# Layer 0's attention over all four quarters as one chain, the following layers behind it by quarters, and layer 2's attention on rows gathered one by one

## The chip, the core and the metric

The kernel runs on one core of one Trainium2 chip. The metric is the device time of one execution in microseconds (us). The kernel before has a median of 2545.66 us over 11 runs (2534.57 to 2553.08).

## The reference

Four layers, each an attention and a feed-forward part, over x of 4 batch rows, 1024 time steps, 128 channels, fp32. Every part is followed by the residual and a layer norm: x = layernorm(x + f(x)). Cut to what the change touches:

```python
def L0_attn(x):                       # a linear attention by cumulative sums over time
    z = causal_conv(x @ in_proj_w) + conv_b              # values, scores, gate
    p_w = exp(clip(score)) * time_weight
    poly = w[0] + w[1]*xv - w[2]*xv**2
    re, im, den = cumsum([p_w*poly*cos(xv*theta), p_w*poly*sin(xv*theta), p_w], axis=time)
    ...                               # / den, rms norm over 2*H*M, W_re, W_im
    return (y * gate) @ out_proj_w
def L0_ffn(x):  return dequant(fp6_blocks32(x)) @ dequant(fp6_blocks32(weight)).T + bias
def L1_attn(x): h[t] = a_disc*h[t-1] + B_disc @ x[t]; return Re(C @ h)      # complex state
def L1_ffn(x):  # 16 experts, 4 per token chosen by groups, beside a shared expert
    return sum_k(tw[k] * expert[idx[k]](x)) + shared(x)
def L2_attn(x): # 16 heads of 8, rotary, softmax over the earlier steps of the same row
    return softmax(mask(q @ k.T)) @ v @ Wo
def L2_ffn(x):  # 8 experts with low-rank additions to common weights, 2 per token
...
```

All that carries over time (the sums of L0_attn, the state of L1_attn, the causal mask of L2_attn) needs earlier steps of the same row first. Routing of a token needs only the token.

## The kernel before

x stays in SBUF as 32 tiles of 128 tokens by 128 channels, ordered by quarter: a quarter is 256 time steps of all four batch rows, 8 tiles. Two quarters are a half.

The program is written as Python generators that issue instructions and yield a nominal duration. `mix(main, side, pace, drain)` (L233) runs two of them against each other: after each step of main it advances side until the nominal times match, and ties each side instruction behind main's latest one on its engine. `press` (L1796) runs a side until something is ready; `chain` and `abreast` put generators one behind the other or next to each other; `all` (L1809) is the order of stages. A scheduler in the framework then fixes the order within each engine. Every engine works through its own list in order and waits at the first instruction that isn't ready. SP issues the plain DMAs in order, POOL the indirect DMAs, in one list with its tensor work.

Stages up to the part that the change leaves alone, in order:

- `l0_attn((0, 1))` (L362): per quarter a projection and convolution on PE, polynomial and phases on DVE and ACT, 9 cumulative scans per quarter on DVE (`l0_scan`, L352), output projection, `norm` (L185). The products with the polynomial run on POOL here (L442), on DVE in quarters 2 and 3 (`no_pool`).
- `l1_setup` (L545), which depends on weights alone, `l2_setup`, `zero_lists` (zero rows to DRAM), and `l0_ffn((0, 1))` (L501) with `quantize` (L473), whose steps alternate DVE and POOL.
- `l1_attn((0, 1))` (L620: projections, two scans, output projection, norm, transposes) beside `l2_weights` (L1385), which builds the 24 weight blocks of the layer-2 experts on PE and stores them to DRAM (`wall2`).
- `l1_route(a)` (L744): scores, top 4, and the position of every token in the lists of its experts (`posl1a`, L1270).
- `l0_attn((2, 3))` beside `spread("l1", a)` (L1305). `spread` is a scatter: for each of 16 tiles and each of its 4 choices one indirect DMA on POOL writes 128 rows of x into the list `l1ra` in DRAM, 64 in all.
- `l1_experts(a)`: 20 groups of 512 list rows are loaded by SP (`xg`), transposed, multiplied by the weights of their expert (`gu`, then `yp`), and stored. `l0_ffn((2, 3))` and `l1_attn((2, 3))` lie beside.
- `l1_shared(a)` and the rest of that side, beside `l1_close(a)` (L825): `collect` (L1348) gathers each token's 4 results (`yt`, indirect DMAs on POOL), adds them, then norm, a store to `xsave`, transposes.
- `l2_attn(0)` (L880), the first half of layer 2's attention by batch rows (`prepare(b)`, scores `sc`, exponentials `pr`, products `s`), beside `l1_route(r)` and `spread("l1", r)` for the second half (list `l1rr`).
- `l1_experts(r)` and `l1_shared(r)` beside `routed(a2)`, layer 2's own routing and scatter (list `l2ra`, 32 scatters); then `l2_experts(a2)` beside `l1_close(r)`; then `l2_attn(1)` and the rest of layers 2 and 3.

The weights of the layer-1 experts, 3 MB (`l1_wall`, L1655), are loaded twice, ahead of `l1_experts(a)` and ahead of `l2_attn(0)`; the second copy stays until `l1_experts(r)` is done.

The core of `spread`, for each tile `t`:

```python
for i in range(k):
    ins = self.indirect(apart=done,
        out=rows, out_offset=bass.IndirectOffsetOnAxis(ap=pos[:, t, i : i + 1], axis=0),
        in_=self.x[:, part.order[t], :], in_offset=None)
```

## Time and profile before

| | |
|---|---|
| median of 11 runs | 2545.66 us (2534.57 to 2553.08) |
| the profiled execution | 2544.01 us |
| its span on the core | 2542.1 us |
| busy: PE, weight loads, DVE, ACT, POOL | 1696.9, 1031.4, 1348.7, 810.7, 779.4 us |
| mean granted TensorE clock | 0.822 |
| HBM read and written | 93.47 and 96.60 MB, 75 GB/s over the span |

Where the stages lie in the trace, by their first and last instructions:

| stage | us from the start |
|---|---|
| `l0_attn` of quarters 0 and 1 | 24 to 154 |
| `l0_ffn` of 0 and 1 | 154 to 207 |
| `l1_attn` of 0 and 1, `l2_weights` | 207 to 285 |
| `l1_route(a)` | 285 to 313 |
| `l0_attn` of 2 and 3, `spread` of `l1ra` | 313 to 428 |
| `l1_experts(a)` | 428 to 541 |
| shared, `l1_attn` of 2 and 3, `l1_close(a)` | 541 to 657 |
| `l2_attn(0)`, `l1_route(r)`, `spread` of `l1rr` | 657 to 921 |
| `l1_experts(r)`, `spread` of `l2ra` | 936 to 1047 |
| `l1_shared(r)` | 1047 to 1089 |
| `l2_experts(a2)`, `l1_close(r)` | 1089 to 1247 |
| `l2_attn(1)` | 1247 to 1660 |
| the rest | 1660 to 2542 |

Busy time is time in which an engine executes something; PE is the matrix engine and PEld its weight loads, DVE the vector, ACT the scalar and POOL the general engine. L12 is line 12 of the kernel before. A name like `gu<-ld,xgT` is what an instruction writes and reads. A wait on "remote" or "another core or an unknown queue" is one whose releaser the profile can't name; there is only one core here.

### The profile page before, as it was taken

The page shows a single profiled execution, that of the slowest core. Times are in us where ns is not written, and L with a number is a line of the kernel's source. Part 1 is how long each engine was busy: PE and PEld are TensorE (multiplying, and loading weights), DVE is VectorE, ACT ScalarE, POOL GpSimd, SP SyncE. Part 2 cuts the span into 40 slices and gives each one's busy share as a digit, 9 for nine tenths or more (in the row PEclk, how much of TensorE's full clock was granted, in tenths as well). Part 3 has the DMA queues.
Part 4 walks back from the last instruction along what each step waited for, and adds up shares of the span by engine and source line. Part 5 has one row for each costly group of instructions (what it writes and reads, how often), then busy time and mean ns, then how long its engine had stood idle before and what let it go on. Part 6 is the DMA issues. An engine that isn't in the chain of part 4 may idle for free.

```text
span 2542.1 us, 28615 instructions
## 1 busy us (share of the span) xinstructions
PE 1696.9 (67%) x9605; PEld 1031.4 (41%) x9605; DVE 1348.7 (53%) x3797; ACT 810.7 (32%) x1158; POOL 779.4 (31%) x725
## 2 busy tenths in 40 slices
PE   7538676873551884797797878768619896754820
PEld 3225333752320353655432332335416684542710
DVE  8864795856460662344546673735403576641453
ACT  5512362311230441222365545512102352310310
POOL 5432185225135004223220001020560203154364
PEclk9768787986785997898898989978859997886965
DMA  9902002341001133322300000030410331221422
GB/s 318 289 14 86 17 35 100 104 133 41 22 25 42 52 120 115 92 60 58 112 24 1 1 3 15 14 126 24 174 58 17 102 108 43 89 87 53 116 79 53
DMA packets 224008, 192.05 MB, mean 76 GB/s; under 512 B 16817, under 2 KB 204081, under 8 KB 222833
## 3 DMA queue, kind: packets, MB, share of 16 engines
q1 hardware_dynamic: 203152, 147.28, 18.4%
q0 software_dynamic: 20704, 42.86, 5.5%
q8 instruction: 83, 1.36, 0.2%
q14 instruction: 69, 0.56, 0.1%
HBM read 93.47 MB, written 96.60 MB: 75 GB/s over the span
## 4 chain that ended last, share of the span: by engine, by line
PE 38%; DVE 15%; another core or an unknown queue 11%; issue 7%; ACT 3%; DMA 2%; POOL 2%; SPq 0%; POOLq 0%; DVEq 0%; ACTq 0%
PE gu L157 10%; PE s L157 8%; PE sc L157 5%; PE yp L157 5%; PE tp L165 4%; PE pu L157 2%; PE pg L157 2%; PE py L157 2%; DVE x L1359 1%; DVE pr L1055 1%; POOL yt L1293 1%; ACT pr L1049 1%; POOL l3rb L1293 1%; DVE x L205 1%
## 5 line engine op out<-in xcount | busy, mean ns | idle before, releaser
L1049 ACT ACTIVATE pr<-sc 128x1024 f32<-128x1024 f32 x288 | 279.5, 1021 | 318.3 <-PE sc L157 200.5
L157 PE MATMUL gu<-ld,xgT 128*128 x768 | 206.6, 412 | 51.7 <-ACT xgT L167 16.9
L157 PE MATMUL s<-pr,va 128*32 128x512 f32 (+3 forms) x1536 | 179.0, 531 | 45.9 <-issue 27.7
L157 PE MATMUL sc<-qm,kT 32*128 32x512 f32 (+3 forms) x1536 | 197.1, 557 | 10.8 <-ACT pr L1049 6.3
L157 PE MATMUL gu<-wall,xgT 128*128 x352 | 181.0, 641 | 20.2 <-DMA wall<-wall 18.2
L157 PEld LDWEIGHTS gu<-ld,xgT 128*128 128x128 f32 x768 | 148.1, 204 | 84.6 <-ACT xgT L167 29.1
L165 PE MATMUL tp<-ld,hg 128*128 128x128 f32 x736 | 117.6, 281 | 90.9 <-DVE hT L169 50.9
L169 DVE COPY hT<-tp 128x512 f32<-128x512 f32 x140 | 96.0, 686 | 139.2 <-remote 68.4
L165 PEld LDWEIGHTS tp<-ld,hg 128*128 128x128 f32 x736 | 93.9, 146 | 149.0 <-issue 62.5
L1689 DVE TENSOR_TENSOR hg<-sg,gu 128x256 f32<-128x256 f32 x192 | 78.5, 417 | 126.2 <-ACT sg L1688 108.5
L1462 ACT ACTIVATE sg<-gu 128x512 f32<-128x512 f32 x88 | 52.5, 597 | 284.4 <-PE gu L157 161.5
L1055 DVE TENSOR_TENSOR pr<-pr,ld 128x512 f32<-128x512 f32 (+1 forms) x160 | 92.4, 580 | 93.1 <-ACT pr L1049 90.5
L157 PEld LDWEIGHTS sc<-qm,kT 32*128 32x128 f32 x1536 | 84.4, 198 | 113.5 <-issue 70.0
L167 ACT COPY xgT<-tp 128x512 f32<-128x512 f32 x118 | 69.1, 586 | 178.0 <-PE tp L165 127.0
L165 PE MATMUL tp<-ld,xg 128*128 128x128 f32 x472 | 77.8, 290 | 69.8 <-ACT hT L167 24.3
L1688 ACT ACTIVATE sg<-gu 128x256 f32<-128x256 f32 x192 | 72.8, 384 | 161.9 <-PE gu L157 111.3
L1464 DVE TENSOR_TENSOR hg<-sg,gu 128x512 f32<-128x512 f32 x88 | 60.1, 682 | 107.6 <-ACT sg L1462 93.1
L1293 POOL DMA_INDIRECT l1ra<-x,posl1a x64 | 93.9, 1468 | 61.0 <-DVE posl1a L1270 41.8
L1293 POOL DMA_INDIRECT yt<-l1yr,posl1r x64 | 60.5, 945 | 152.7 <-DVE x L1359 79.5
L157 PE MATMUL yp<-ld,hT 128*128 x768 | 103.1, 276 | 3.6 <-DVE hT L169 3.3
L157 PEld LDWEIGHTS s<-pr,va 128*32 128x32 f32 x1536 | 38.8, 113 | 157.1 <-issue 111.2
L157 PE MATMUL yp<-wall,hT 128*128 x704 | 98.2, 285 | 1.5 <-DVE hT L169 1.5
(433 smaller groups left out, 3531.9 us busy)
## 6 DMA issues: line engine op xcount, KB each, us to landing
wall<-wall SPq DMA_DIRECT2D x16, 768.0 KB
l3ra<-zero SPq DMA_DIRECT2D x1, 6144.0 KB
wall<-we SPq DMA_DIRECT2D x24, 256.0 KB
ld<-in_l_w SPq DMA_DIRECT2D x2, 3072.0 KB
ld<-in_l_w SPq DMA_DIRECT2D x1, 6144.0 KB
xg<-l3ra SPq DMA_DIRECT2D x24, 256.0 KB
l3ya<-yg SPq DMA_DIRECT2D x24, 256.0 KB
l1ra<-zero SPq DMA_DIRECT2D x1, 5120.0 KB
```

Source lines behind the costliest of these rows:

```text
L157: return self.nc.tensor.matmul(out, lhsT, rhs, start=start, stop=stop)
L165: nc.tensor.transpose(pt[:, k * P : (k + 1) * P], s, self.ident)
L167: nc.scalar.copy(dst, pt[:, : n * P])
L169: nc.vector.tensor_copy(dst, pt[:, : n * P])
L205: nc.vector.tensor_scalar(x, x, mv[:, t, 0:1], rstd[:, t : t + 1], ALU.subtract, ALU.mult)
L1049: nc.scalar.activation(pr, sc[h], AF.Exp)
L1055: nc.vector.tensor_tensor(d, d, cst["tril"].unsqueeze(1).unsqueeze(1).to_broadcast([P, 2, n, P]), ALU.mult)
L1293: ins = self.nc.gpsimd.indirect_dma_start(**kw)
L1462: nc.scalar.activation(sg, gu[:, 0, :], AF.Silu)
L1464: nc.vector.tensor_tensor(h, sg, gu[:, 1, :], ALU.mult)
L1688: nc.scalar.activation(sg, pg[:, :, 0, :], AF.Silu)
L1689: nc.vector.tensor_tensor(h[:, 2 * c : 2 * c + 2, :], sg, pg[:, :, 1, :], ALU.mult)
```

## The change

- `l0_attn` runs once, over all four quarters. Its products run on POOL in quarters 0 to 2 and on DVE in quarter 3. Behind each quarter of it, and beside the next, come `l0_ffn` and `l1_attn` of the same quarter (`after`, `then`); `l1_setup`, `l2_setup` and `zero_lists` come behind quarter 0.
- After `l1_attn` of quarter 1 comes `l1_route(a1)`, then `spread` of it abreast with `l0_ffn` and `l1_attn` of quarters 2 and 3 and `l1_route(r)`.
- What of that is left over runs beside `l2_weights`, which has its scaled copy `am` made by ACT in place of POOL. Then `l1_shared(a1)` and `l1_experts(a1)` run beside `spread` of `r`.
- `l2_attn(0)` runs beside `l1_close(a1)`, which now goes by batch rows: four tiles are gathered, added, normed, stored and transposed, and the row is listed. `prepare(b)` presses the side until its row is listed. `l1_close(r)` goes by rows too, beside `l2_experts(a2)` as before.
- The second load of the layer-1 weights comes after `l2_attn(0)`.
- The scaling of the norms of layer 0 and of `l1_attn` is on ACT (`on_act`); the reciprocal root of the `l0_ffn` and `l1_attn` norms is always on DVE. `im` and `re` take the place of `t` and `k`, three buffers each. Some pools have fewer buffers or lie on another side of SBUF.

```diff
@@ -122,7 +122,7 @@
         self.lists, self.route = {}, {}
-        self.both = (self.first, Part("r", 2, 2))
+        self.both = (Part("a", 0, 2, range(B)), Part("r", 2, 2, range(B)))
         for lay, ne, k in (("l1", E1, K1), ("l2", E2, K2), ("l3", E3, K3)):
...
@@ -201,8 +202,14 @@
                 self.rsqrt(rstd, ve)
+        if on_act:
+            off = self.tile(self.small, [P, n], f"off{n}")
+            nc.vector.scalar_tensor_tensor(off, mv[:, :, 0], -1.0, rstd, ALU.mult, ALU.mult)
         for t, x in enumerate(tiles):
-            nc.vector.tensor_scalar(x, x, mv[:, t, 0:1], rstd[:, t : t + 1], ALU.subtract, ALU.mult)
+            if on_act:
+                nc.scalar.activation(x, x, AF.Identity, bias=off[:, t : t + 1], scale=rstd[:, t : t + 1])
+            else:
+                nc.vector.tensor_scalar(x, x, mv[:, t, 0:1], rstd[:, t : t + 1], ALU.subtract, ALU.mult)
...
@@ -411,9 +418,9 @@
                 ts(pq, xv, self.nw2, self.dw[:, 1:2], ALU.mult, ALU.add)
-                times(pq, pq, xv, ALU.mult)
+                times(q)(pq, pq, xv, ALU.mult)
                 nc.vector.scalar_tensor_tensor(pq, pq, self.dw[:, 0:1], pwx, ALU.add, ALU.mult)
-                den = self.tile(bp, [P, QC], "den")
+                den = self.tile(bp, [P, QC], "den", bufs=1)
                 self.l0_scan(den, pwx, 2 * MF, q)
...
@@ -428,18 +435,18 @@
-                    t = self.tile(tp, [P, QC], "t")
-                    nc.scalar.activation(t, xv, AF.Copy, scale=self.turn[:, m : m + 1])
-                    k = self.tile(tp, [P, QC], "k")
+                    turn = self.turn[:, m : m + 1]
+                    t = self.tile(tp, [P, QC], "t", bufs=3)
+                    nc.scalar.activation(t, xv, AF.Copy, scale=turn)
+                    k = self.tile(tp, [P, QC], "k", bufs=3)
                     ts(k, t, RND, None, ALU.add)
                     nc.vector.scalar_tensor_tensor(k, k, RND, t, ALU.subtract, ALU.subtract)
-                    im = self.tile(tp, [P, QC], "im")
+                    im, re = t, k
                     nc.scalar.activation(im, k, AF.Sin, scale=-2.0 * PI_IN)
                     nc.scalar.activation(k, k, AF.Abs)
-                    re = self.tile(tp, [P, QC], "re")
                     nc.scalar.activation(re, k, AF.Sin, scale=-2.0 * PI_IN, bias=self.halfpi)
                     for part, v in ((1, im), (0, re)):
-                        times(v, v, pq, ALU.mult)
+                        times(q)(v, v, pq, ALU.mult)
                         s = self.tile(tp, [P, QC], "s", bufs=3)
...
@@ -466,7 +473,8 @@
                     tt(x[:, t0 : t0 + 4, :], po, x[:, t0 : t0 + 4, :], ALU.add)
-                self.norm(self.quarter(q), by="act" if no_pool else "pool")
+                self.norm(self.quarter(q), by="act" if q in no_pool else "pool", on_act=True)
+                self.listed.add(f"l0 {q}")
                 yield (10.0,)
...
@@ -520,7 +527,7 @@
                 )
-                yield (10.0,)
+                yield (13.0,)
...
@@ -660,7 +667,7 @@
-                (tt if beside else nc.gpsimd.tensor_tensor)(rows(g[0]), rows(g[0]), steps(pw[:, 0, :]), ALU.mult)
+                tt(rows(g[0]), rows(g[0]), steps(pw[:, 0, :]), ALU.mult)
                 tt(rows(g[1]), rows(g[1]), steps(pw[:, 1, :]), ALU.mult)
...
@@ -671,17 +678,17 @@
                     yield (3.0,)
-                self.norm(self.quarter(q), by="dve" if beside else "act")
+                self.norm(self.quarter(q), by="dve", on_act=True)
                 yield (6.0,)
-    def logits(self, pl, wr, t0, nt):
-        for t in range(nt):
-            self.mm(pl[:, t, :], self.xT[:, (t0 + t) * P : (t0 + t + 1) * P], wr)
+    def logits(self, pl, wr, tiles):
+        for i, t in enumerate(tiles):
+            self.mm(pl[:, i, :], self.xT[:, t * P : (t + 1) * P], wr)
...
@@ -824,16 +831,21 @@
-        nc, x = self.nc, self.x
-        for q in range(part.q0, part.q0 + part.nq):
-            yield from self.collect("l1", part, K1, yp, (q - part.q0) * QT, QT)
-            self.norm(self.quarter(q))
-            tl = slice(q * QT, (q + 1) * QT)
-            nc.sync.dma_start(out=self.xsave[:, tl, :], in_=x[:, tl, :])
-            yield (6.0,)
-            for g in range(2):
-                self.turned(self.side, q * QT + g * 4, tag="s")
-                yield (1.5,)
+        nc, x, hf = self.nc, self.x, part.q0 // 2
+        xTv = self.xT.rearrange("p (q b t) -> p b q t", q=NQT, b=B)
+        for b in range(B):
+            yield from self.collect("l1", part, K1, yp, b * 4, 4)
+            tiles = part.order[b * 4 : b * 4 + 4]
+            self.norm([x[:, t, :] for t in tiles], by="dve")
+            for t in tiles[::2]:
+                nc.sync.dma_start(out=self.xsave[:, t : t + 2, :], in_=x[:, t : t + 2, :])
+            yield (5.0,)
+            pt = self.tile(self.side, [P, BLK], "s")
+            for k, t in enumerate(tiles):
+                nc.tensor.transpose(pt[:, k * P : (k + 1) * P], x[:, t, :], self.ident)
+            nc.vector.tensor_copy(xTv[:, b, 2 * hf : 2 * hf + 2, :], pt.rearrange("p (q t) -> p q t", q=2))
+            self.listed.add(f"row {hf}{b}")
+            yield (2.0,)
...
@@ -909,6 +921,7 @@
+                self.press(side, lambda: f"row {hf}{b}" in self.listed)
                 qT = self.tile(bp, [P, BLK], "qT")
...
@@ -1387,16 +1400,18 @@
         with ExitStack() as ctx:
-            cp = self.pool(ctx, "l2wc", right=True)
-            wp = self.pool(ctx, "l2ww", 3, right=True)
+            cp = self.pool(ctx, "l2wc")
+            wp = self.pool(ctx, "l2ww", 3)
             big = self.load(cp, self.ins["l2_big"])
             ab = self.load(cp, self.ins["l2_ab"])
+            em = self.tile(cp, [P, E2], "em2")
+            nc.vector.tensor_scalar(em, self.cst["em"], 2.0, None, ALU.mult)
             yield (0.0,)
                     am = self.tile(wp, [P, P], "am")
-                    nc.gpsimd.tensor_scalar(am, ab[:, i, :], self.cst["em"][:, e : e + 1], 2.0, ALU.mult, ALU.mult)
+                    nc.scalar.activation(am, ab[:, i, :], AF.Copy, scale=em[:, e : e + 1])
                     pw = self.tile(self.side, [P, F2], "s")
...
@@ -1409,7 +1424,7 @@
                     nc.sync.dma_start(out=self.wall2[:, c0 : c0 + F2], in_=we)
-                    yield (1.0,)
+                    yield (2.5,)
...
@@ -1754,6 +1769,16 @@
+    def after(self, q):
+        yield from self.when(lambda: f"l0 {q}" in self.listed)
+        if q == 0:
+            self.l1_setup()
+            yield (20.0,)
+            self.l2_setup()
+            self.zero_lists("l1")
+            yield (4.0,)
...
@@ -1818,38 +1843,37 @@
                 self.l2_wr = self.load(lgp, self.ins["l2_wr"])
-                self.run(self.l0_attn((0, 1)))
-                self.l1_setup()
-                self.l2_setup()
-                weights = self.l2_weights()
-                next(weights)
-                self.zero_lists("l1")
-                self.run(self.l0_ffn((0, 1)))
-                self.run(self.mix(self.l1_attn((0, 1)), weights))
-                self.run(self.l1_route(a))
-                self.run(self.mix(self.l0_attn((2, 3), True), self.spread("l1", a, K1)))
+                main = self.l0_attn(range(NQT), (NQT - 1,))
+                then = lambda q: self.chain(self.after(q), self.l0_ffn((q,)), self.l1_attn((q,)))
+                side = self.chain(
+                    then(0), then(1), self.l1_route(a1),
+                    self.abreast(self.spread("l1", a1, K1), self.chain(then(2), then(3), self.l1_route(r))),
+                )
+                self.run(self.mix(main, side, pace=0.8, drain=False))
                 self.zero_lists("l2", "l3")
+                self.run(self.mix(self.l2_weights(), side))
                 with ExitStack() as c2:
                     wall = self.l1_wall(c2)
-                    yp = self.pool(c2, "l1ya", 5, right=True)
-                    side = self.chain(self.l0_ffn((2, 3), True), self.l1_attn((2, 3), True))
-                    self.run(self.mix(self.l1_experts(a, wall), side, drain=False))
-                    self.run(self.mix(self.chain(self.l1_shared(a), side), self.l1_close(a, yp)))
+                    side = self.spread("l1", r, K1)
+                    self.run(self.mix(self.chain(self.l1_shared(a1), self.l1_experts(a1, wall)), side))
+            with ExitStack() as c2:
+                yp = self.pool(c2, "l1ya", 5, right=True)
+                side = self.l1_close(a1, yp)
+                self.run(self.mix(self.l2_attn(0, side), side))
             with ExitStack() as c2:
                 wall = self.l1_wall(c2)
-                self.run(self.mix(self.l2_attn(0), self.chain(self.l1_route(r), self.spread("l1", r, K1))))
                 wall2 = self.l2_wall(c2)
                 self.run(self.mix(self.chain(self.l1_experts(r, wall), self.l1_shared(r)), self.routed(a2)))
-                self.run(self.mix(self.l2_experts(a2, wall2), self.l1_close(r, yp)))
+                side = self.l1_close(r, yp)
+                self.run(self.mix(self.l2_experts(a2, wall2), side))
             listed = lambda name: lambda: name in self.listed
             )
-            self.run(self.mix(self.l2_attn(1), on, drain=False))
+            self.run(self.mix(self.l2_attn(1, on), on, drain=False))
             with ExitStack() as c3:
```

The lines left out pass these things through: pool sides and names, `side` PSUM in place of own pools in `l0_ffn` and `l1_attn`, the logits by the part's tile order.

## The prediction

> **What bounds the kernel now.** I read the page's slices and chain first, then windows by stage, then the groups of the three scatter tiles, then the waits of the one stretch where all engines stand still.
>
> ```profile
> PE   7538676873551884797797878768619896754820
> DVE  8864795856460662344546673735403576641453
> POOL 5432185225135004223220001020560203154364
> PE 38%; DVE 15%; another core or an unknown queue 11%; issue 7%; ACT 3%; DMA 2%; POOL 2%; SPq 0%; POOLq 0%; DVEq 0%; ACTq 0%
> ```
>
> A slice is 63.6 us. No engine is full for long: stages with different limits follow each other. The thirteenth slice (763 to 826) has PE 1, DVE 0. "Unknown queue" holds 11% of the chain. The windows are columns of time, length, then busy us and count for PE, weight loads, DVE, ACT, POOL, then granted clock, DMA share, GB/s:
>
> ```profile
> 24.00:154.00 130.00, 85.14 (x347) 37.85 (x345) 104.07 (x118) 66.60 (x81) 57.26 (x24) 0.80 0.85 241
> 154.00:207.00 53.00, 16.12 (x69) 12.46 (x69) 34.52 (x93) 5.20 (x11) 20.21 (x11) 0.60 0.00 0
> 313.00:428.00 115.00, 78.25 (x340) 36.56 (x336) 100.55 (x146) 59.23 (x68) 93.51 (x64) 0.81 0.14 52
> 541.00:657.00 116.00, 42.92 (x161) 27.15 (x161) 60.26 (x220) 10.08 (x17) 65.98 (x64) 0.63 0.26 82
> 745.00:822.00 77.00, 9.73 (x36) 3.07 (x28) 1.93 (x7) 2.22 (x3) 51.31 (x54) 0.52 0.12 46
> 921.00:1047.00 126.00, 85.47 (x533) 74.33 (x525) 56.68 (x213) 36.62 (x74) 30.65 (x32) 0.86 0.45 147
> ```
>
> Rows 1 and 3 are l0_attn, bound by DVE. Rows 2 and 4 (l0_ffn; l1_shared, l1_attn(2,3), l1_close) are chains that fill no engine; the change wants to put these under other work. Row 5 is l2_attn(0) while spread(r) scatters: the core stands still. The groups of the scatters, l1ra (beside l0_attn(2,3)), l1rr (beside l2_attn(0)), l2ra (beside l1_experts(r)):
>
> ```profile
> L1293 POOL DMA_INDIRECT l1ra<-x,posl1a x64: 954/1043/3016, 312.6 to 424.8; - x64
> L1293 POOL DMA_INDIRECT l1rr<-x,posl1r x64: 954/958/1113, 731.7 to 811.5; - x64
> L1293 POOL DMA_INDIRECT l2ra<-x,posl2a x32: 954/958/982, 956.3 to 995.5; - x32
> ```
>
> Min/median/max ns, then first and last start. l1ra is stretched to (424.8-312.6)/63 = 1.78 us apart and costs its neighbour nothing; l1rr goes at (811.5-731.7)/63 = 1.27 us and stops everything from 745 to 822. The chain and the waits of 740 to 830 name it:
>
> ```profile
> 761.94 59.93 another core or an unknown queue
> ACT pr L1049 <- remote: 73.7, 2, 71.9
> DVE t L169 <- remote: 60.0, 1, 60.0
> ```
>
> l2ra does the same to the experts: 20 groups of l1_experts(r) take 936.2 to 1046.8 = 110.6 us, at 3.54 us a group in the undisturbed part plus 5 us run-in (76), so 32 scatters lose 34 us, about 1.1 each. l3ra (64, some 70 us lost) agrees. Two things set l1ra apart, and the trace can't part them: DVE is 99% busy from 330 to 400, and few instructions run (340 matmuls in 115 us against 533 in 126).
>
> **The change part by part.** I carry all to one mark: the first gu matmul of l1_experts(r), at 936.2 before. What comes after holds the same work (row-wise l1_close(r) and pressed waits in l2_attn(1) I put at 0, from -10 to +10: l1_close(r) lay beside l2_experts, PE 137.04 of 158 us, and still does).
>
> 1. *To posl1a.* The first quarter of l0_attn is alone as before and ends near 117. From there to posl1a (L1270), the list positions that the scatters need, the built order has 232 us of DVE work by median row durations, row by row. In parts, which come to 237: three quarters of l0_attn (45 each: scans L358 2.3, L435 1.6), l0_ffn and l1_attn of quarters 0 and 1, route(a1) (windows: 34.5+35.2+23.2 = 93), l1_setup, which lay in DVE's idle prologue (+15), g[0] on DVE (L663; 1.2 each), rsqrt on DVE (+9), less the norm scalings that go to ACT (L205, 2.14 per quarter, 8 quarters = 17). POOL's multiplies stretch DVE: in 24 to 154 the DVE rows sum to 111.6 us where their medians give 90.8. q1 and q2 keep them: +20. At 97% busy: 117 + 252/0.97 = 377; I take 375 (355 if inflation is nil and packing full, 397 if DVE is busy only 90%). Before: 312.3. The routing comes 63 us later because l0_attn(2,3) now lies ahead of it.
>
> The Trainium skill, "SBUF — State Buffer", section "Who interferes with whom", speaks against POOL multiplies beside a full DVE: the pair of ports that the two share is an exclusive lock, and the loser waits for the whole instruction. Were POOL's 57.26 us in the first window all lost to DVE, the +20 would be some +57; the measured inflation, 20.8 us, decides here. The same section says TensorE and ScalarE never wait for that lock, which taken alone would price the scatters at nothing for PE and give the fast rival below; the fifth window has PE at 9.73 of 77 us, so the measurement differs and decides.
>
> 2. *spread(a1).* POOL is in order. Its queue holds 21 scatters mixed with quantize(2) of l0_ffn, then 43 in a row, and only then quantize(3). 64 x 1.26 = 81 us, +10 for quantize(2)'s POOL rows (L485 2.2, L495 2.4, L497 2.4, L525 2.6), up to +10 for the rest of l0_attn on DVE: it ends at 466 to 476. Before, it lay wholly under l0_attn(2,3).
>
> 3. *What waits behind it.* quantize(3), stuck behind the 43, 16 to 21 us; l0_ffn(3)'s matmuls 14; norm and transposes 16; l1_attn(3) 30 (before, L641 to L672 per quarter). On PE the gu of l1_experts(a1) stand behind l1_attn(3) and route(r)'s logits. So the first gu is some 78 after 468 = 546 if nothing freezes. If the 43 freeze the tail (norms, l1_attn(2), l2_weights, whose 65 us of PE were to be filler here), 574: 28 of the 47 us they can take are on that chain. I take 562, the middle and 2 for the landing of the last scatter; before, 438.1.
>
> 4. *l1_experts(a1) beside spread(r).* 76 as above, + 64 scatters at 2 x 34 = 68, + 5 for posl1r at its head: 149. Without a freeze 85. On SP its first xg load, which waits for all of l1ra, stands ahead of six of the 24 stores of wall2 (L1411), and the 3 MB wall load behind the second group's; wall2 is read only at the mark, so the stores cost 0, and a late wall 0 to +10, in the range.
>
> 5. *Row 0 of l1_close(a1)* is pressed before l2_attn(0)'s first prepare, so nothing covers it: landing 2.3 + 16 gathers at 1.25 = 20, + adds, norm, transposes 3 to 12, + 11 to the first sc: 36. The other rows lie beside attention.
>
> 6. *l2_attn(0).* Before 668.8 to 921 = 252; less the 77 us stall that leaves it = 175; +10 for row closes on DVE (L1359, L205) = 185.
>
> 7. *To the mark.* 15 us tail as before (921 to 936.2), plus the wall: its SBUF is free only when l2_attn(0) ends, while before it was loaded ahead; 3 MB at the 14.20 us the later wall load shows: +15. In all 30. The 6 MB of wall2 follow behind it on SP; xg loads queue with it: 0 to +10.
>
> Sum: 562 + 149 + 36 + 185 + 30 = 962 against 936: **+26**. Said as a ledger: the experts start 124 us later (562 against 438), and from there to the mark takes 400 instead of 498. The profiled execution took 2544.0 (span 2542.1), 1.7 below the median of the runs; 2545.7 + 26 gives 2571 or 2572; I write 2571.
>
> The rest at 0: norm scalings and am on ACT (L1688's 128x256 takes 0.384 us, so eight 128x128 take at most 3.1 against DVE's 2.14; ACT is busy 59 of 115 us in l0_attn, 10 of 116 in the chains); sin and cos in place with three buffers, same instructions; tiles in another order in logits, lists and closes; xsave in 16 stores of 2 tiles, SP being idle; l2_attn's transposed rows copied by DVE (L169, 0.7 us each, inside term 6). If ACT were the bound the norms would cost 1 us a quarter.
>
> **The rivals.**
>
> A, *no freeze: faster.* The freeze is tied to what l2_attn and the experts happened to do; scatters run stretched beside the tail and beside the experts as l1ra did. Then 546 + 85 + 36 + 185 + 30 = 882, -54: 2491. For: l1ra's 64 without loss; l2_weights fills PE. Against: l2ra froze this very expert loop. Half of it (only spread(r) freezes, 546 + 149) is +10: 2556. It turns to a gain when the first gu comes before 536 with spread(r) frozen, or 600 without.
>
> B, *both freeze whole, POOL's queue decides: slower still.* 574 + 149 + 36 + 185 + 30 = 974, +38: 2584; with DVE only 80% busy as in the first window (104.07 of 130), posl1a comes at 117 + 252/0.8 = 432, all of 57 later: up to 2640. For: that window is the only stretch with POOL multiplies. Against: it waited for loads (DMA share 0.85), and side work fills later gaps.
>
> C, *the wall load is not exposed and rows close under cover:* SP prefetches, pressing finds row 0 ready: -30, 2541, no change within the noise.
>
> **How the numbers follow.** Forecast (partly frozen, 2550 to 2600): 0.42. B beyond 2600: 0.14. A (2470 to 2530): 0.28. C and mixtures (2530 to 2550): 0.16, of which 0.06 lies within 0.2% (5 us, about what a measurement here can tell), 0.06 below, 0.04 above. So faster 0.34, same 0.06, slower 0.60. The range leaves out the faster end of A (0.10) and the slower end of B (0.09): 2485 to 2620; the forecast's own is 2550 to 2600.
>
> **What would show it.** posl1a between 355 and 397; the last l1ra scatter near 470 with qt of quarter 3 right behind it on POOL; first gu of gu<-ld,xgT near 562; a window over l1rr with PE under 2 tenths beside the experts; l2_attn(0) without a still stretch, some 185 long; a wait on the wall near 15 us ahead of l1_experts(r). Wrong, if scatters in the tail or in the experts stand 1.7 us or more apart with PE busy, or if DVE has gaps of 20% in l0_attn. Stages behind the mark that differ by over 10 us would be a cause I haven't priced.

## The result and the profile after

The changed kernel takes 2696.8 us (median of 8 runs, 2689.3 to 2700.6) against 2544.6: a ratio of 1.0591, interval 1.0574 to 1.0609. The forecast was slower by 26 us, with a range up to 2620; it is slower by 152. The profiled execution took 2699.1, its span is 2697.3.

The slices of the page after (67.4 us each; the rows are PE, DVE, POOL):

```profile
PE   7666542683535677478779788867836898564720
DVE  6998762553244666234453666453711377550453
POOL 4533028205342100422331001002162201335264
PE 40%; DVE 21%; another core or an unknown queue 17%; issue 10%; POOL 5%; ACT 3%; DMA 3%; SPq 0%; DVEq 0%; POOLq 0%; ACTq 0%
```

The hole that lay in slice 13 of the kernel before is now spread over slices 7 (404 to 472), 10 and 12. In the chain the unknown queue rose from 11% to 17%. By windows (columns as before: us, then busy and count of PE, weight loads, DVE, ACT, POOL, clock, DMA share, GB/s), cut at the terms of the sum:

```profile
117.00:391.00 274.00, 167.48 (x699) 87.37 (x698) 220.65 (x530) 111.70 (x163) 60.66 (x24) 0.79 0.06 18
390.00:483.00 93.00, 14.99 (x50) 10.46 (x50) 23.31 (x58) 5.41 (x12) 73.69 (x68) 0.52 0.11 45
483.00:597.00 114.00, 94.84 (x399) 58.70 (x400) 61.54 (x172) 45.23 (x101) 9.12 (x5) 0.89 0.28 99
597.00:768.00 171.00, 82.76 (x477) 73.08 (x477) 58.58 (x210) 35.51 (x72) 61.91 (x64) 0.73 0.26 81
768.00:845.00 77.00, 11.52 (x20) 4.59 (x20) 25.50 (x87) 0.00 (x0) 49.47 (x52) 0.52 0.19 50
845.00:1033.00 188.00, 139.06 (x1164) 66.04 (x1165) 121.47 (x349) 75.70 (x78) 13.42 (x12) 0.85 0.08 27
```

In order: l0_attn behind its first quarter, with the layers beside it, up to the first scatter; spread(a1), with PE 15 of 93; the tail to the experts' first gu; l1_experts(a1) with spread(r) in it, PE 83 of 171; the exposed close of row 0, PE 12 of 77; l2_attn(0), no longer with a still stretch. The scatters' groups (min/median/max ns, first and last start):

```profile
L1306 POOL DMA_INDIRECT l1ra<-x,posl1a x64: 954/958/1973, 390.6 to 482.2; - x64
L1306 POOL DMA_INDIRECT l1rr<-x,posl1r x64: 954/958/1199, 621.5 to 701.7; - x64
```

l1ra's median is down from 1043 ns to 958: beside l0_attn they were held apart, here they go back to back. The waits from 620 to 715, beside spread(r), look like those of the still stretch before, at a new place:

```profile
DVE hg L1704 <- ACT sg L1703: 55.3, 3, 43.8
PEld gu L157 <- issue: 42.7, 2, 37.8
ACT sg L1703 <- remote: 34.7, 4, 12.9
```

PE's longest wait is for nothing that the profile can name ("issue"), ACT waits for an unnamed releaser, and DVE for ACT. The scatters themselves are not late: the first packet of most of l1rr's comes 1.54 us after the issue, in the middle of the stop as at its ends, and 2.6 us at most.

### The profile page after: what moved, and what is told of

Its sections match the earlier page's. It is cut to its first block, busy times and chain, and to the rows that moved or that the text cites. A ratio compares the mean times of both kernels' runs of the same rounds, so it can differ in the third digit from the quotient of the medians.

```text
span 2697.3 us, 28800 instructions
## 1 busy us (share of the span) xinstructions
PE 1725.5 (64%) x9605; PEld 1046.9 (39%) x9605; DVE 1378.1 (51%) x3887; ACT 839.9 (31%) x1254; POOL 762.4 (28%) x709
## 4 chain that ended last, share of the span: by engine, by line
PE 40%; DVE 21%; another core or an unknown queue 17%; issue 10%; POOL 5%; ACT 3%; DMA 3%; SPq 0%; DVEq 0%; POOLq 0%; ACTq 0%
PE gu L157 11%; PE s L157 10%; PE sc L157 5%; PE yp L157 5%; PE tp L165 4%; POOL yt L1306 2%; DVE s L365 2%; PE pu L157 1%; DVE x L1372 1%; PE pg L157 1%; DVE bn L192 1%; POOL l3rb L1306 1%; ACT pr L1062 1%; DVE pr L1068 1%
## 5 line engine op out<-in xcount | busy, mean ns | idle before, releaser
L157 PE MATMUL sc<-qm,kT 32*128 32x512 f32 (+3 forms) x1536 | 203.1, 574 | 12.8 <-issue 8.0
L157 PE MATMUL s<-pr,va 128*32 128x512 f32 (+3 forms) x1536 | 170.8, 526 | 14.1 <-DVE x L1000 5.3
L1479 DVE TENSOR_TENSOR hg<-sg,gu 128x512 f32<-128x512 f32 x88 | 59.9, 682 | 102.6 <-ACT sg L1477 89.7
L1306 POOL DMA_INDIRECT yt<-l1ya,posl1a x64 | 62.9, 983 | 138.9 <-issue 83.4
L157 PE MATMUL yv<-s,wbd 128*128 128x512 f32 x128 | 73.5, 701 | 40.6 <-DVE s L365 23.3
```

The source lines that it names most:

```text
L157: return self.nc.tensor.matmul(out, lhsT, rhs, start=start, stop=stop)
L1306: ins = self.nc.gpsimd.indirect_dma_start(**kw)
L1479: nc.vector.tensor_tensor(h, sg, gu[:, 1, :], ALU.mult)
```

## The experiments

### The same scatters left out of both kernels

In `spread`, the inner loop runs over nothing for the named lists; all else stays. First group of runs:

```diff
-            for i in range(k):
+            for i in range(0 if lay + part.name in ('l1a', 'l1r',) else k):    # a_no_both, b_no_both
+            for i in range(0 if lay + part.name in ('l1r',) else k):           # a_no_r
```

> The changed kernel with the 64 scatters of spread(r) left out (its list stays zero; every other instruction stays). Theory 1, scatters issued back to back stop the other engines: l1_experts(a1) took 171 us from its first gu matmul (596.8) to the first gather (768.0) where 20 groups at 3.54 us and 5 us of run-in are 76; with 5 us for the routing at its head, 90 us go: 2697 - 90 = 2607 us (2595 to 2620), and the window of the experts has PE at 8 tenths or more throughout. Theory 2, the loss lies in the new order (POOL's queue, row 0 of the close, the late wall), and the scatters fill time in which the experts wait for something else: less than 20 us go, 2680 to 2697.

> The changed kernel with the 128 scatters of spread(a1) and spread(r) left out. Theory 1: the 90 us of spread(r), and with spread(a1) gone quantize of quarter 3 no longer stands behind 64 scatters on POOL and nothing stops: the first gu matmul comes some 100 us after posl1a at 390 (end of l0_attn, quantize 19, matmuls 14, norm and transposes 16, l1_attn 30, logits and load 15), near 495 in place of 597; 2697 - 90 - 100 = 2507 us (2490 to 2530). Theory 2: l2_weights and the chain of quarter 3 fill that time anyway, and the first gu comes no earlier than 560; 2640 to 2660.

> The kernel before with the same 128 scatters left out, so that the two orders can be compared without them. Theory 1: l1ra's 64 cost nothing beside l0_attn(2,3) and l1rr's 64 cost the still stretch in l2_attn(0): 2544 - 75 = 2469 us (2458 to 2482). Theory 2, the still stretch is a wait for something that the scatters only accompany: 2535 to 2545. The difference to the changed kernel without them is what the order costs by itself: 38 us by theory 1, 100 or more by theory 2.

Measured, one run each: 2261.4, 2223.9 and 2157.4, where the kernel before took 2165.7 on that chip, some 380 below its executions on every other. Nothing stops there. l2ra's 32 scatters beside l1_experts(r), in b_no_both on that chip and then in the kernel before (b_same) on the next one:

```profile
851.00:892.00 41.00, 38.14 (x242) 34.51 (x243) 19.95 (x46) 17.52 (x37) 31.12 (x32) 0.96 0.66 199
```
```profile
954.00:995.00 41.00, 15.06 (x69) 11.98 (x69) 5.11 (x15) 4.47 (x9) 30.74 (x32) 0.74 0.35 113
```

POOL does the same (32 in 41 us, 31 busy); PE is busy 38 us on one chip and 15 on the other, and 15.8 in b_no_both2 further down, the program of the first row on a chip with the stop. So the program alone does not make the stop. Whether it is the chip or the moment these runs can't tell: all that lack it are of one group on one chip. My numbers had supposed a stop that is absent there, so the expectations of these three failed. What they do give is that the order has a price without any stop, 2223.9 - 2157.4 = 66 us, and that spread(a1) has one too: 2261.4 - 2223.9 = 37.5 us. Its scatters, and the first POOL step of quantize for the four quarters, with them (a_no_r) and without (a_no_both):

```profile
L1306 POOL DMA_INDIRECT l1ra<-x,posl1a x64: 955/962/2412, 388.8 to 483.3; - x64
L493 POOL TENSOR_TENSOR qt<-x,qri x4: 1912/1920/1926, 133.3 to 484.3; 128x1024 f32<-128x1024 f32 x4
```
```profile
L493 POOL TENSOR_TENSOR qt<-x,qri x4: 1909/1911/1912, 132.5 to 447.3; 128x1024 f32<-128x1024 f32 x4
```

quantize(3) starts right behind the last scatter, 37 us later than without, and the first gu comes 35 us later (577.4 against 541.9). That is POOL's queue, as step 3 of the prediction had it, with no engine stopped. All later groups fell on chips with the stop (before: 2544.2 to 2547.1), where I repeated the pair:

> The changed kernel without its 128 scatters of layer 1, on this chip. With the freeze: 2690 less the 95 us that l1_experts(a1) lost and less 35 to 100 us from spread(a1) to the first gu: 2495 to 2560. Its distance to the kernel before without the same scatters is the price of the order: 66 on the chip without a freeze (2223.9 against 2157.4), so 50 to 90 here. Without the freeze: 2220 to 2228 again.

> The kernel before without the same 128 scatters, on this chip. With the freeze: 2544 - 75 - 9 = 2460 (2450 to 2475), the 9 being what they cost where nothing stops (2165.7 against 2157.4). Without: 2155 to 2160.

2549.6 and 2462.2: **the order costs 87 us, with no layer-1 scatter in either.** The scatters cost 2547.1 - 2462.2 = 85 in the kernel before. In the changed one they cost 138: it stands 140.6 above the kernel before with them (a_same, below) and 2.6 without. 87 + 53 = 140. These are single runs, and the kernel before alone spreads from 2534.6 to 2553.5 over 31, so each of these differences is known to some 10 us.

Where the two kernels without scatters part (from their traces, changed against before): first gu 539.4 against 434.9; first sc of l2_attn(0) 707.5 against 663.9, +44; its last sc +64; last store of l1_experts(r) +71; first sc of l2_attn(1) 1265.7 against 1178.9, +87; after that nothing.

### The changed kernel on a chip with the stop, and two single edits

> The kernel before itself, to have its trace on this chip. If there is no freeze: 2160 to 2170, with l1rr's 64 scatters dense (1.26 us apart) and PE over 7 tenths busy beside them. If there is: 2535 to 2555 and the still stretch of 75 us.

> The changed kernel itself, beside the kernel before on the same chip. The first group of runs showed the kernel before at 2165.7 us with no still stretch around its scatters, 379 us below the recorded executions. If this chip is like that one: theory 1 (the freeze is the chip's or the moment's, the order has a price of its own) says the changed kernel is near a_no_r's 2261, since spread(r) then lies under the experts: 2255 to 2285, ratio 1.04 to 1.055. Theory 2 (the loss is the freeze) says a ratio of 0.98 to 1.02. If this chip is like the recorded one: 2690 to 2700, ratio 1.059.

2546.8 for the kernel before, and 2685.1 for the changed one (ratio 1.0554, 1.052 to 1.0589), close to the recorded result. Which scatters cost what: with and without them, the first gu comes at 593.1 and 539.4 (+54; in the kernel before 440.8 and 434.9, +6), and from there to the last store of l1_experts(a1) it takes 166.7 and 87.3 (+79; in the kernel before l2_attn(0) carried +78). So spread(r) costs the same at either place, and 48 of the extra 53 are spread(a1), which lost its cover.

```diff
 a_qdve:  -  nc.gpsimd.tensor_tensor(...)    # L493, L503, L505, L532
          +  (nc.gpsimd if q < 2 else nc.vector).tensor_tensor(...)
 a_muls:  -  main = self.l0_attn(range(NQT), (NQT - 1,))
          +  main = self.l0_attn(range(NQT), (1, 2, 3))
```

> The changed kernel with the POOL steps of l0_ffn (three in quantize, one bias add) on DVE for quarters 2 and 3, so that POOL has nothing behind or between the 64 scatters of spread(a1). Theory 1 (the chain of quarter 3 waits in POOL's queue): the scatters end 64 x 1.27 = 81 us after posl1a in place of 92 to 95, quantize(3) runs during them, and the first gu comes 40 to 75 us earlier without a freeze; with the freeze 10 to 30 us earlier, since the chain stands still anyway. Theory 2 (the tail is bound by DVE and by the 65 us of PE work of l2_weights): within 10 us of the changed kernel.

2692.3 in a single run: no gain. The scatters end 7 us sooner (474.4 against 481.6), but the first gu is at 596.9 against 593.1. With the stop POOL's queue does not decide: in the changed kernel POOL stands idle for 18.5 us behind the last scatter, until DVE has done its part of quantize(3) ("POOL qt L493 <- DVE qri L490: 18.5"). Queue and stop overlap: where nothing stops, the queue alone makes 35 of the 54 us.

> The changed kernel with the 18 products of quarters 1 and 2 of l0_attn on DVE in place of POOL (9 per quarter, 1.21 us each on DVE by the row of L442 = 22 us more DVE work, less the 20 us of inflation that I put on DVE for them). Theory 1 (POOL's products stretch DVE as much as they save): posl1a within 10 us of the changed kernel's and the time within 10 us. Theory 2 (POOL's products are nearly free): 15 to 25 us slower.

2680.1 in a single run, within what a_same's runs spread over (2677.0 to 2693.9), but the first scatter comes at 372.4 in place of 388.9. The windows up to the experts' first gu, by which both have done the same work, a_same and a_muls:

```profile
0.00:593.00 593.00, 352.86 (x1426) 187.81 (x1426) 396.53 (x853) 226.73 (x351) 202.42 (x133) 0.77 0.30 93
```
```profile
0.00:579.00 579.00, 347.13 (x1427) 188.22 (x1428) 386.53 (x871) 229.81 (x355) 142.36 (x113) 0.78 0.31 96
```

DVE does 18 products more, 22 us by their rows, and is busy 10 us less. So the 18 products on POOL, 52 us by their rows there, stretched DVE by about 32. Theory 1, and beyond it: for DVE they cost more than they saved. The rule of the Trainium skill, "SBUF — State Buffer", section "Who interferes with whom", on the exclusive lock between the two engines would, taken as a loss of all their time, give 52; the measured 32 lies between that and my +20.

### Scatters held apart

A power of a tiny tile after each scatter keeps POOL from issuing the next one; it is tied behind the scatter, and the next scatter behind it (cut to the loop; `slow` says whether the list is one of those held apart, `nap` is the last power):

```diff
                 done.append(ins)
+                if slow:
+                    if nap is not None:
+                        self.tc.add_manual_dep(ins.ins, nap.ins.name, behind, reason="paced")
+                    nap = self.nc.gpsimd.tensor_tensor(self.idle, self.idle, self.mhalf[:, :4], ALU.pow)
+                    self.tc.add_manual_dep(nap.ins, ins.ins.name, behind, reason="paced")
-            yield (1.26 * k,)
+            yield ((2.4 if slow else 1.26) * k,)
```

> The kernel before with all 64 scatters of spread(r), each followed on POOL by a tiny power of 4 elements per partition, so that they go some 2.2 to 2.6 us apart (the nominal step of spread is raised to 2.4 to match). Theory 1a, only scatters issued back to back stop the engines: 64 x 2.4 = 154 us lie beside the 175 us of l2_attn(0), no still stretch, 2544 - 70 = 2474 us (2462 to 2490). Theory 1b, each scatter costs the others about 1.1 us whatever the distance: 2540 to 2555.

2205.3, on the chip without the stop, which both theories miss; it decides nothing, as told in the next one:

> The kernel before with l1rr's 64 scatters held 2.4 us apart by a tiny POOL power after each, again, since the first such run fell on a chip where back-to-back scatters stop nothing (2205.3 against 2165.7 for the kernel before: there the longer spread only ended 41 us after the attention). On a chip with the freeze (before near 2545): theory 1a, only back-to-back scatters stop the engines: l2_attn(0) has no still stretch and the spread ends some 40 us after it: 2544 - 75 + 41 = 2510 (2495 to 2525). Theory 1b, each scatter costs some 1.1 us at any distance: 2560 to 2590.

2508.2. l2_attn(0) with l1rr beside it, in b_same and in b_pace_r2:

```profile
730.00:812.00 82.00, 17.77 (x96) 6.80 (x96) 14.24 (x49) 3.99 (x4) 61.62 (x64) 0.57 0.13 51
```
```profile
730.00:835.00 105.00, 85.42 (x785) 42.23 (x788) 75.11 (x204) 48.36 (x50) 95.08 (x88) 0.93 0.15 60
```

POOL is busier (91% against 75%) and PE goes from 2 to 8 tenths. So it is not POOL's being busy that stops the core, nor does it take a full DVE to prevent it (DVE is at 72% here and was at 99% beside l1ra); it is indirect DMAs issued one right behind the other. Theory 1a holds at 2.4 us. The power brings two things at once, a longer distance and another instruction between the scatters, and no run parts them; l1ra, 1.78 us apart in the kernel before with nothing between, costs only 6 us, which speaks for the distance; but DVE is nearly full there, so it proves nothing. Then all scatters, then a shorter distance (a power of 1 element in place of 4, nominal 1.8):

> The same distance for every scatter of the kernel before (l1ra, l1rr, l2ra, l2rm, l2rn, l3ra, l3rb, l3rc: 320 in all). With the freeze: theory 1a, some 24 + 34 + 70 + 66 + 75 us of stops go and the longer spreads push what waits for them: l1ra ends 40 us after l0_attn(2,3), l1rr 40, the others lie under experts: 2450 to 2520. Theory 1b: 2580 to 2650. Without the freeze: 2240 to 2300.

2521.8, just above its range: what the missing stops save is partly given back by l1ra, which now ends some 60 us later (487.5 against 425.8 in b_pace_r2), in front of the experts.

> The same short distance for l1rr alone. With the freeze, theory 1a: 64 x 1.75 = 112 us, the spread ends at 842 with the attention (835): 2506 - 35 = 2471 (2462 to 2485). If 1.7 us is too dense: a still stretch of some 40 us or more in l2_attn(0) and 2500 to 2550. Without the freeze: 2166 to 2180.

2474.5. The group: distance (845.4 - 724.8)/63 = 1.91 us, and no stop.

```profile
L1295 POOL DMA_INDIRECT l1rr<-x,posl1r x64: 991/1028/1477, 724.8 to 845.4; - x64
```

> The kernel before with a POOL power of 1 element per partition after every scatter but l1ra's, whose stretch beside l0_attn(2,3) costs nothing as it is: distance some 1.6 to 1.9 us (nominal 1.8). From the page's stages with 2.4 us everywhere: the stages behind l1_experts(r) took 1575 us in place of 1617, and the shorter distance lets l1rr's spread end with the attention. With the freeze: theory 1a, back-to-back is what stops the engines and 1.7 us is enough: 2506 - 42 - 35 = 2429 us (2405 to 2460), faster than both kernels. Rival, the freeze begins below 2 us: 2490 to 2545. Without the freeze: 2185 to 2210.

**2375.8 us, ratio 0.9334 (0.9316 to 0.9352): faster than both kernels**, with the stages of the kernel before and nothing changed but the distance of 256 scatters and the nominal step that goes with it. It came below the forecast 2405: l3ra's stretch, for one, has PE busy 87.78 of 117 us, where b_same has 44.51 of 88.

> The changed kernel with the short distance (power of 1 element) for both of its layer-1 spreads. With the freeze, theory 1a: l1_experts(a1) takes 90 us in place of 167 beside spread(r): 77 us go; spread(a1) ends 64 x 0.5 = 32 us later, at 512, and l0_ffn(3) with it, but its neighbours no longer stand still: first gu between 580 and 615. In all 2685 - 77 +- 20 = 2590 to 2630, still slower than the kernel before. If the order alone were to blame, 2700 or more. Without the freeze: 2270 to 2300.

2678.4 in a single run: the mechanism held and the forecast failed. The first gu comes at 618.4, just behind its range. The experts beside the paced spread(r) take 85 us (618.4 to 703.5), no stop; the two windows behind each other:

```profile
620.00:708.00 88.00, 74.68 (x475) 67.54 (x473) 56.20 (x201) 33.31 (x70) 58.61 (x73) 0.93 0.47 139
708.00:755.00 47.00, 0.00 (x0) 0.00 (x0) 0.00 (x0) 0.00 (x0) 41.26 (x52) 0.50 0.09 37
```

In the second only POOL works: the rest of spread(r), ahead of row 0's gathers in its queue, to 757.9. Where they are dense the scatters stop the core; where they are not, the queue does. That is the trap of the changed order: l1_close(a1) stands behind spread(r) on POOL.

### The exposed close, and the place of spread(r)

```diff
-                    self.x[:, part.order[t], :], yt[:, i, :], wk[:, t, i : i + 1], self.x[:, part.order[t], :],
+                    self.x[:, part.order[t], :], self.zero if lay + part.name == 'l1a' else yt[:, i, :], wk[:, t, i : i + 1], self.x[:, part.order[t], :],
...
-            for i in range(k):
+            for i in range(0 if lay + part.name == 'l1a' else k):
                 self.indirect(
```

> The changed kernel without the 64 gathers of l1_close(a1): the adds take zeros in their place, so the routed experts of the first half are missing from x; every other instruction stays. Tells what row 0's press is made of (77 us from the first gather to the first sc where I had put 36). Theory 1, the gathers are the wait and, back to back, slow DVE (the window 800 to 850 has DVE busy 16.2 of 50): first sc some 30 to 35 us after the experts end, rows 1 to 3 free of it: 45 to 60 us less, 2625 to 2640 with the freeze. Theory 2, the chain of adds, norm, transposes and prepare on DVE sets it: 15 to 25 us less, 2660 to 2670. Without the freeze: 2261 - 25 to 35 = 2226 to 2236 by theory 1.

2613.5 in a single run, 12 below the range of theory 1. From the last store of the experts to the first sc it takes 24 us (760.3 to 784.5) in place of 81 (759.8 to 840.6), and the attention is 15 shorter. Theory 1: the gathers are 57 of the 81. Only 20 of those are row 0's 16 issues; 52 gathers go out in a row, and the window 768 to 845 above has PE at 11.5 and DVE at 25.5 of 77. The gathers slow the others as well, less sharply: from the first gather to the first sc it takes 50 us in a_no_both, on the chip without the stop, and 77 in a_no_both2, the same program on a chip with it.

> The changed kernel with three things mended: the POOL steps of l0_ffn for quarters 2 and 3 on DVE, a POOL power of 1 element after every scatter of both layer-1 spreads (distance 1.85 us), and spread(r) moved from l1_experts(a1) to l2_attn(0), behind the gathers of l1_close(a1) on POOL. With the freeze: first gu near 550 (540 is what the chain takes without any scatter), experts 88, first sc 77 after the first gather = 715 to 725, attention 190, spread(r) done with it, first gu of l1_experts(r) near 930, and 1632 from there as in a_pace1: 2562 us (2540 to 2580). That would put the whole extra loss of 50 to 60 on the scatters' place and distance, and leave the order's 87 over the kernel before with its l1rr paced (2474.5 + 87 = 2561). If it stays over 2620, something else than scatters and order is at work. Without the freeze: 2225 to 2245.

```diff
-                    side = self.spread("l1", r, K1)
-                    self.run(self.mix(self.chain(self.l1_shared(a1), self.l1_experts(a1, wall)), side))
+                    self.run(self.chain(self.l1_shared(a1), self.l1_experts(a1, wall)))
...
-                side = self.l1_close(a1, yp)
+                side = self.chain(self.l1_close(a1, yp), self.spread("l1", r, K1))
```

(with a_qdve's edit and the short distance on both spreads). 2579.9, ratio 1.0139 (1.0117 to 1.0161), at the edge of what was expected. Of the 141 us above the kernel before 36 are left; it stands 105 above the kernel before with its own l1rr paced, where the order's 87 was expected. The first gu came at 581 and not 550; the waits of 460 to 510 say why:

```profile
PEld py L159 <- DVE hs L746: 39.7, 1, 39.7
DVE x L832 <- DMA l1ra<-x,posl1a: 39.4, 1, 39.4
```

l1_shared(a1) adds into the x tiles that spread(a1) is still reading. Its add (L822 of the kernel before, L829 of the changed one) stands in DVE's queue, and with it all of quarter 3. A wait that the changed order makes possible and the old one, with the shared expert behind the experts, never had. In the changed kernel itself it does not show: its first such add comes at 521.6, after the last scatter.

> The changed kernel with l1_close(r) by quarters as before (norm, one store to xsave and transposes by ACT per quarter; r's tiles in quarter order), all else as changed. The stretch from the first gu of l2_experts(a2) to the first sc of l2_attn(1) took 193 us in the changed kernel and 173 in the one before (1209.4 to 1402.7 against 1089.6 to 1262.3). Theory 1, the row-wise close makes that: 12 to 20 us less, ratio 1.048 to 1.054 on a chip with the freeze. Theory 2, it comes from where the gathers now fall between the expert groups: ratio 1.054 to 1.060.

```diff
-        self.both = (Part("a", 0, 2, range(B)), Part("r", 2, 2, range(B)))
+        self.both = (Part("a", 0, 2, range(B)), Part("r", 2, 2))
...
+        if part.name == "r":
+            for q in range(part.q0, part.q0 + part.nq):
+                yield from self.collect("l1", part, K1, yp, (q - part.q0) * QT, QT)
+                self.norm(self.quarter(q))
...
+            self.listed |= {f"row {hf}{b}" for b in range(B)}
+            return
         for b in range(B):
```

Ratio 1.0462 (1.0437 to 1.0487) against a_same's 1.0554 (1.052 to 1.0589): 0.9% or some 23 us, and the stretch in question takes 174.0 us (1211.2 to 1385.2) against 193.3. Theory 1, a little beyond its upper edge: the row-wise close of r costs what l2_experts(a2) beside it does not hide.

## Why the prediction was wrong

The sign was right, as were the two mechanisms it named first (the experts start much later; spread(r) stops them). The size was not: +26 forecast, +152 measured, and no single term makes the difference. By its terms, in the recorded trace:

| step | predicted | measured |
|---|---|---|
| first scatter | 375 | 390.6 |
| first gu of l1_experts(a1) | 562 | 596.8 |
| to the first gather | 149 | 171.2 |
| row 0 of the close | 36 | 77.3 |
| l2_attn(0), first to last sc | 185 | 188.0 |
| to the mark | 30 | 21.6 |
| mark | 962 | 1054.9 |
| behind the mark | 0 | +27.5 |

- **The mark itself.** I took 936.2 for the first gu of l1_experts(r), from the chain; the trace of before has it at 927.2. Counted alike the mark moved by 127.7. 9 us of the miss were there before any step, and the 34 us that l2ra loses rest on the same start. They hold all the same: l1_experts(r) takes 119 us in b_same and 86 in b_no_both, where nothing stops.
- **Step 1, +16.** Two errors against each other: DVE was busy 220.65 us in that stretch and not 252, but in 274 us, 81% and not 97%. The 80% that rival B took from the first window was the right packing. POOL's products stretched DVE by some 32 us and not 20 (a_muls), so it was the other rows that I had counted too high.
- **Steps 2 and 3, +19 more.** From the first scatter to the first gu I had 187 us: 171 without a stop, and 16 for half of one and the last landing. It took 206.2. Where nothing stops the same stretch takes 188.6 (a_no_r, 388.8 to 577.4), so the stop's part, about 17 us, was near the 14 that I gave it, and the 171 was some 18 short: the chain behind the scatters is longer than the 78 I had for it. The total came out like rival B's whole stop, for another reason. (The two chips may be compared here: without the scatters the first gu comes at 541.9 on one and 539.4 on the other.) quantize(3) behind the scatters, my reason for the chain, holds where nothing stops (35 us); with the stop, taking it off POOL gains nothing (a_qdve). Without any layer-1 scatter the first gu still comes at 539 (a_no_both2, PE busy 106 of the 150 us from 389 on). spread(a1), which before cost 6 us beside a full DVE, cost 54 on top.
- **Step 4, +22.** Right mechanism, mis-sized: 64 scatters lost 79 us beside the experts (a_same against a_no_both2), where twice l2ra's 34 gave 68; from the first gu to the last store without them is 87, where I had 76 + 5.
- **Step 5, +41, the largest miss.** I priced only row 0's 16 gathers, and the other rows' at nothing. 52 went out in a row, and DVE and PE were slow while row 0's adds, norm and prepare were due (without gathers 57 us less, a_no_gath).
- **Step 6** held (+3). The gathers of the other rows make 15 us of it (a_no_gath), where I had 10 for the row closes. **Step 7** was 8 too dear: PE's wait for the wall ahead of the first gu is 2.1 us and not 15. But in the kernel before the experts began 10 us after the last sc, ahead of the attention's last matmuls, and now 21.6 after it.
- **Behind the mark, +27.5 for 0.** 19 of it is l1_close(r) by rows (a_close_q): l2_experts(a2), with PE at 137 of 158, was no cover. Why it was none is argued at most: PE being nearly full, a step of the close that holds it up adds to the time. Another 11 come behind the first sc of l2_attn(1), 9 of them in l2_attn(1); a_same and b_same do not repeat those (362 and 366 us there).
- **Rival A** (the moved scatters stop nothing, -54) did not come: PE is at 15 of 93 us beside spread(a1) and at 15 of 88 beside spread(r) (a_same, 620 to 708). Nor could it have: without one layer-1 scatter the changed kernel still takes 2549.6 against 2547.1 for the kernel before with all of them. And where nothing stops the kernel before has no still stretch to lose: the changed order, rid of spread(r), took 2261.4 there against 2165.7.

The order's 87 us by the traces without scatters: 44 up to the first sc of l2_attn(0), 21 in it (row closes beside it; the gathers are 15 of such a stretch by a_no_gath), 7 to the end of l1_experts(r), 16 from there to the first sc of l2_attn(1), which r's row-wise close accounts for (a_close_q). What remains argued and not shown is how the first 44 divide between the serial tail (l2_weights and l1_shared now in front of the experts) and the exposed row 0.

## What to carry to other kernels

Work moved off one engine's idle time takes its queue with it: ask for every moved DMA what then stands behind it on its issuing engine, and which tiles it still reads when the next writer comes. Before pricing a reordering, price the stall that is there: this change carried a stop of some 75 us to another place, while in the kernel before a tiny instruction after each of 256 scatters takes 7% off the time with no new order at all. A sum over a chain should take the packing of the busiest engine from a window of the same kind, not from the best one.

## What the runs showed of the hardware that was not expected

- Indirect DMAs issued by POOL 1.26 us apart stop PE, ACT and DVE (PE 17.8 of 82 us in b_same); with a tiny POOL instruction between them, 1.8 to 1.96 us apart, they do not (in b_pace_best 89.7 of 109 in l2_attn(0), and 57.3 of 62 beside l2ra), though POOL is busier. Where between 1.3 and 1.8 it turns, no run shows. The first packets come as soon after the issue in the stop as outside it, so it is not a backlog of transfers; what holds the engines is open. They are not quite still: from 768 to 785 in b_same PE gets one matmul through every 2.80 us, each after 2.43 us of waiting for nothing that the trace names.
- On one of the five chips that the experiments fell on, back-to-back scatters stopped nothing and the kernel before took 2165.7 in place of 2545. No run tells why, nor whether it is the chip or the moment.
- 18 products on POOL, 52 us there, beside a nearly full DVE stretched DVE's other work by some 32 us.
